# A split that keeps its first half in DRAM, and a close that loads it

## The chip, the cores and the metric

The kernel runs on one core of one Trainium2 chip. The metric is the device time of one launch in microseconds (us), lower is better; runs of one kernel are compared by their median.

## The reference, cut to what matters

The input is four images of 96 channels by 128 x 128 pixels (NCHW, float32). Layer 0 is a group norm followed by a selective-scan block (a 1 x 1 convolution to 192 channels, a depthwise 3 x 3, SiLU, four scans in different directions, a layer norm over channels, a 1 x 1 convolution back), added to the input. Layer 1 is the part that the change touches:

```python
def _relu_split_norm(x, sc1, sc2, res_coef, nc1, nc2):
    x = x - mean(x);  x1 = relu(x);  x2 = x - x1
    ...                                   # masks, pos, neg, avg1, avg2
    x1n = sqrt(pos/total) * _layer_norm(x1 + avg1 * downmask)
    x2n = sqrt(neg/total) * _layer_norm(x2 + avg2 * upmask)
    out = 0.5 * (nc1 * x1n + nc2 * x2n) + res_coef * x
    return (out, sc1 * x1 + x1n, sc2 * x2 + x2n)

xr, x1, x2 = _relu_split_norm(_gn(x), ...)
y1 = _layer_norm(_attn_conv(x1, x2, aw1, aw2, aw3))
y2 = _layer_norm(_conv2d(x2, w_conv2, 1)) * x1
x = x + xr + _conv2d(concat([y1, y2]), w_full, 0) + b_full
```

`_attn_conv` makes keys from `x1`, queries from `x2`, a softmax over them as 3 x 3 convolution weights, and convolves a value map of `x1` with those. The first half `x1` is so needed twice: as the input of the convolutions, and at the end as the factor of `y2`.

## The kernel before

The scans of layer 0 come first. After them the images go one by one through four steps, each a Python generator that emits instructions and yields the cost it estimates for them:

- `norm`: the end of layer 0 for the image. It writes the image's new `x` to DRAM (`xnew`, 96 x 16384) in 16 pieces of 96 x 1024.
- `split` (`split_norm`): loads `xnew` once for the sums, then again in 16 pieces. For each piece and each half, ScalarE makes scale times x plus shift (L1253) and VectorE masks it by the threshold `thr` (L1257). For images 1 to 3 the result stands in a tile `half` of 8 rows x 4 column groups x 33 (32 pixels and one pad of zero, 96 x 1056 floats; two tiles for the first half, one for the second). From it six planes are made on ScalarE and GpSimd (first half) or VectorE (second half) and stored to `x1p` and `x2p`. Only the planes are kept, not the half. For image 0 the two halves themselves are stored, as maps with one pad per row of 129 (`x1d`, `x2d`). There the pixels stand in plain order; the planes of the other images split a row into four groups of 32, and all that follows for them stands in that order (`img.mapped` tells the two apart).
- `attend`: the convolutions and the attention of the image, in strips of 12 rows on TensorE (`products`, L1467 and L1482), with ScalarE copies (L1540, L1928) and VectorE combinations (L1554 to L1562). It stores the `w_conv2` convolution to `c2d` and the attention's output to `od`. Its inputs `ya`, `yc` are loaded two strips ahead (L1903, L1911).
- `close` (`attn_output`): 16 pieces of 96 x 1024. It loads `od` (tile `o`), `c2d` (tile `c2`) and `xnew` (tile `xx`) one piece ahead, makes the first half again from `xx` in tile `x1` (`first_half`: L2273 on ScalarE, L2274 on VectorE), forms (c2 - mean) * x1 in place (L2316), makes the residual `e` (`residual`: L2278 on ScalarE, L2279 and L2280 on VectorE), multiplies both by the 1 x 1 weights (L2324, L2325), adds `e` into `x1` (L2327 or L2329) and stores `x1` to the output (L2331). Every tile of it has two buffers.

`co_run(left, right, pace)` interleaves the emission of `attend` (left) with a chain of lighter work (right): beside `attend` of image b run `norm` and `split` of image b+1 and `close` of image b-1. Beside the last image runs `close` of image 2 with its yields doubled, and then `LastOutput`, which does for image 3 what `close` does in three steps. `before` makes `x1` and `e` of image 3 from `xnew` and stores both (`x1s`, `es`); `beside` loads them with `c2d` and adds the second product into a tile that stays; `after` adds the first product and stores the output.

All loads and stores named here are issued by SyncE (SP), in its program's order, except the stores of `x1d` and `x2d`. After the scans, the order of instructions on each engine is that of a scheduler in the framework, which moves instructions of attention, split and close past each other; within an engine each instruction waits for its place in that order.

Of the kernel before, what the change touches and what calls it, by code (L numbers as in the profile page):

```python
# [9 lines left out]
F32 = mybir.dt.float32  # L10
BF16 = mybir.dt.bfloat16
AF = mybir.ActivationFunctionType
ALU = mybir.AluOpType
# [4 lines left out]
C = 96  # L18
H = W = 128
L = H * W  # L20
# [9 lines left out]
PW = W + 1  # L30
TW = 4
NP = TW + 2
TN = W // TW
PB = TN + 1
PP = PB * TW
# [18 lines left out]
SN = 1024  # L54
NS = L // SN
RS = SN // W
# [15 lines left out]
def kernel(  # L72
# [26 lines left out]
    nc = tc.nc  # L99
# [4 lines left out]
    dram = ctx.enter_context(tc.tile_pool(name="dram", bufs=2, space=DRAM))  # L104
# [983 lines left out]
                    nc.sync.dma_start(xnew[:, bass.ts(old, SN)], near.pop(old)[turned])  # L1088
                yield 1.4

    def split_norm(xnew, x1d, x2d, stats, keep, cnt, ps, side, planes, vector, done):


        with ExitStack() as pools:
            p4 = pools.enter_context(tc.tile_pool(name="n4", bufs=3, side=side))
            ahead = []
# [13 lines left out]
            m = col("m1")  # L1110
# [12 lines left out]
            t = col("t1")  # L1123
# [6 lines left out]
            later = Later()  # L1130
            p1 = ExitStack()
            p2 = p1.enter_context(tc.tile_pool(name="n1", bufs=2, side=side))
            for i in range(NS):
                y = ahead.pop(0)
# [80 lines left out]
            def stored(i, m, h):  # L1215
                if planes:
                    def then(pl):
                        store_planes(nc.sync, m, i * RS, RS, pl)
                        done[m is x2d] = (i + 1) * RS

                    return planes_of(later, p2, h, RS, then, vector=vector(i, m is x2d))
                at = (i * RS + 1) * PW
                return lambda: nc.scalar.dma_start(m[:, at : at + RS * PW], h)

# [1043 lines left out]
        nc.gpsimd.memset(y[C : C + 1], 1.0)  # L2268
        return y[0 : C + 1]

    def first_half(img, xx, x1):
        thr, scale, shift = (img.keep[n] for n in ("thr", "scale", "shift"))
        nc.scalar.activation(x1, xx, AF.Identity, scale=scale[:, 0:1], bias=shift[:, 0:1])  # L2273
        nc.vector.scalar_tensor_tensor(x1, xx, thr, x1, ALU.is_gt, ALU.mult)  # L2274

    def residual(img, xx, e):
        up, low, thr = (img.keep[n] for n in ("up", "low", "thr"))
# [4 lines left out]
    def pixels(v):  # L2282

        return v.rearrange("p (h j t) -> p h t j", j=TW, t=TN)

    def plain(v):
        return v.rearrange("p (h t j) -> p h t j", j=TW, t=TN)

    def attn_output(img, ps, side, share):
        ob = out[img.b].rearrange("c h w -> c (h w)")  # L2290
        with (
            tc.tile_pool(name="f1", bufs=1, side=side) as p1,
            tc.tile_pool(name="f3", bufs=2, side=side) as p3,
        ):
            w1 = own_weights(img, ps, p1)
            s2, w2 = c2_weights(img, ps, p1)
            ones = [with_ones(p1, f"o{i}") for i in range(2)]

            def loads(t):
                o = ones[t % 2]  # L2300
                got = [o]
                nc.sync.dma_start(o[0:C], img.od[:, bass.ts(t, SN)])
                for name, src in (("c2", img.c2d), ("xx", img.xnew)):
                    y = p3.tile([C, SN], F32, name=name)
                    nc.sync.dma_start(y, src[:, bass.ts(t, SN)])
                    got.append(y)
                return got

            ahead = loads(0)
            for t in range(NS):  # L2310
                o, c2, xx = ahead
                if t + 1 < NS:
                    ahead = loads(t + 1)
                x1 = p3.tile([C, SN], F32, name="x1")
                first_half(img, xx, x1)
                nc.vector.scalar_tensor_tensor(  # L2316
                    c2, c2, s2[0:C, 0:1], x1, ALU.subtract, ALU.mult
                )
                e = p3.tile([C, SN], F32, name="e")
                residual(img, xx, e)  # L2320
                for h in range(2):
                    sl = bass.ts(h, CH)
                    pf = part(ps, C, CH)
                    nc.tensor.matmul(pf, lhsT=w1, rhs=o[:, sl], start=True, stop=False)  # L2324
                    nc.tensor.matmul(pf, lhsT=w2, rhs=c2[:, sl], start=False, stop=True)  # L2325
                    if img.mapped:
                        nc.vector.tensor_add(x1[:, sl], pf, e[:, sl])  # L2327
                    else:
                        nc.vector.tensor_add(plain(x1[:, sl]), pixels(pf), pixels(e[:, sl]))  # L2329
                    yield 2.6 * share  # L2330
                nc.sync.dma_start(ob[:, bass.ts(t, SN)], x1)  # L2331

    class LastOutput:

# [3 lines left out]
        def __init__(self, img, ps, side):  # L2338
            self.img, self.ps, self.side = img, ps, side
            self.pools = ExitStack()  # L2340
            self.kept = None
            self.x1d, self.ed = (dram.tile([C, L], F32, name=n, bufs=1) for n in ("x1s", "es"))

        def open(self):
            pool = self.pools.enter_context(tc.tile_pool(name="o3", bufs=1, side=self.side))
# [3 lines left out]
        def before(self):  # L2349

            img = self.img
            self.open()
            with tc.tile_pool(name="f3", bufs=2, side=self.side) as p3:
                def load(t):
                    y = p3.tile([C, SN], F32, name="xx")
                    nc.sync.dma_start(y, img.xnew[:, bass.ts(t, SN)])
                    return y

                ahead = load(0)
                for t in range(NS):  # L2360
                    xx = ahead
                    if t + 1 < NS:
                        ahead = load(t + 1)
                    x1, e = (p3.tile([C, SN], F32, name=n) for n in ("x1", "e"))
                    first_half(img, xx, x1)
                    yield 4.0
                    residual(img, xx, e)
                    yield 5.2
                    for d, y in ((self.x1d, x1), (self.ed, e)):
                        nc.sync.dma_start(d[:, bass.ts(t, SN)], y)  # L2370

        def beside(self):

            img = self.img
            while self.kept is None:
                yield None
            with (
                tc.tile_pool(name="f1", bufs=1, side=self.side) as p1,
                tc.tile_pool(name="f3", bufs=2, side=self.side) as p3,
            ):  # L2380
                s2, w2 = c2_weights(img, self.ps, p1)

                def loads(t):
                    got = []
                    for name, src in (("c2", img.c2d), ("x1", self.x1d), ("e", self.ed)):
                        y = p3.tile([C, SN], F32, name=name)
                        nc.sync.dma_start(y, src[:, bass.ts(t, SN)])
                        got.append(y)
                    return got

                ahead = loads(0)
                for t in range(NS):
                    c2, x1, e = ahead
                    if t + 1 < NS:
                        ahead = loads(t + 1)
                    nc.vector.scalar_tensor_tensor(
                        c2, c2, s2[0:C, 0:1], x1, ALU.subtract, ALU.mult
                    )
                    for h in range(2):
                        sl = bass.ts(h, CH)  # L2400
                        pf = part(self.ps, C, CH)
                        nc.tensor.matmul(pf, lhsT=w2, rhs=c2[:, sl], start=True, stop=True)
                        nc.vector.tensor_add(
                            plain(self.kept[:, t, sl]), pixels(pf), pixels(e[:, sl])
                        )
                        yield 2.2
# [29 lines left out]
    class Image:  # L2436


        def __init__(self, b):
            self.b = b  # L2440
            self.xnew = dram.tile([C, L], F32, name="xnew", bufs=3)
            self.x1p, self.x2p, self.vp = planes[b % 2]
            self.x1d, self.x2d, self.vd = maps if b == 0 else (None, None, None)
            self.stats = istats[b % 2].tile([C, NCH, 6], F32, name="xstats", tag="xstats")
            self.cnt = istats[b % 2].tile([C, 5, NS], F32, name="cnt", tag="cnt")
            self.keep = {}
            self.mapped, self.lifting = False, False
            self.done = [0, 0]
            self.finished = False
            self.last = None  # L2450
            self.maps_made = lambda: None
            self.watd = None if b else dram.tile([C, 3, NP, C], F32, name="watd", bufs=1)
# [13 lines left out]
        def split(self, ps, side, vector=lambda i, second: False):  # L2466
            halves = (self.x1p, self.x2p) if self.b else (self.x1d, self.x2d)
            yield from split_norm(
                self.xnew, *halves, self.stats, self.keep, self.cnt, ps, side, self.b > 0, vector,
                self.done,  # L2470
            )

# [215 lines left out]
```

## Time and profile before

| | |
|---|---|
| median of 3 runs | 6464.88 us (6458.56 to 6468.28) |
| time of the profiled execution | 6470.83 us |
| its span, first to last instruction | 6468.9 us |
| TensorE matmul (PE) busy | 5321.3 us, 82% |
| VectorE (DVE) busy | 4711.2 us, 73% |
| ScalarE (ACT) busy | 3786.8 us, 59% |
| GpSimd (POOL) busy | 3238.6 us, 50% |
| DMA | 1205.18 MB, 186 GB/s |
| mean granted TensorE clock | 0.889 |

Busy time is the sum of the times of an engine's instructions; the idle time of an engine is put down to the instruction or transfer that ended it. "DMA share" is the mean busy share of the 16 DMA engines in a stretch, and GB/s is what they moved in it. The granted clock is a share of the full one. A share over the whole span is a mean over stages of very different kind, so the stages are read one by one.

### The profile page before, as it was taken

Reading aid. Unit: us, or ns where it says so; the run is one execution under the profiler, and the core shown is the slowest. Engines: PE = TensorE matmul, PEld = TensorE weight load, DVE = VectorE, ACT = ScalarE, POOL = GpSimd, SP = SyncE. Lnnn points to the kernel's source line nnn. Section 1 sums busy time; section 2 is a strip of 40 time slices with the busy share of each in tenths; the row PEclk is TensorE's granted clock in tenths of the full one; section 3 lists DMA queues with packets and bytes.
Section 4 is the critical chain, followed back from the end, with each engine's and each line's share of the span. In section 5 each row is a group of like instructions: output and inputs, shape, how many; then the busy total and the mean of one; then the engine's idle time right before and its main releaser. Section 6 shows DMA issues by size and latency. Waiting matters only on the chain. (4 is left out here: it accounts for less than half of the span.)

```text
span 6468.9 us, 76257 instructions
## 1 busy us (share of the span) xinstructions
PE 5321.3 (82%) x23264; PEld 2301.3 (36%) x23264; DVE 4711.2 (73%) x7132; ACT 3786.8 (59%) x4770; POOL 3238.6 (50%) x2472
## 2 busy tenths in 40 slices
PE   6889988987888753989988588877888877989888
PEld 2333323322222111444433234345333445345553
DVE  4247778988989668988934785468874587888757
ACT  1247767776787676777632565466533665545642
POOL 1226757978889544979821344346213266022310
PEclk9999989998998665999999799888988988999989
DMA  6767777775675766675666776665766655966668
GB/s 154 176 157 193 191 202 196 218 213 163 199 198 163 214 173 215 197 217 174 199 182 185 187 220 161 164 157 155 213 195 164 178 145 155 243 174 181 191 170 219
DMA packets 891433, 1205.18 MB, mean 186 GB/s; under 512 B 228533, under 2 KB 743483, under 8 KB 878545
## 3 DMA queue, kind: packets, MB, share of 16 engines
q1 hardware_dynamic: 860496, 1145.35, 65.2%
q0 software_dynamic: 16208, 38.41, 2.2%
q10 hardware_dynamic: 14320, 16.54, 0.9%
q8 instruction: 187, 3.06, 0.2%
q14 instruction: 222, 1.81, 0.1%
HBM read 777.82 MB, written 345.62 MB: 174 GB/s over the span
## 5 line engine op out<-in xcount | busy, mean ns | idle before, releaser
L629 PE MATMUL bank<-y,wp 128*128 128x512 f32 (+3 forms) x3584 | 1320.2, 626 | 84.5 <-DMA y<-y 40.9
L862 POOL TENSOR_TENSOR y<-y,dl 128x1024 f32<-128x1024 f32 x384 | 1062.5, 2767 | 273.1 <-DVE dl L854 247.9
L829 POOL TENSOR_TENSOR dl<-dl,u 128x1024 f32<-128x1024 f32 x384 | 1015.8, 2645 | 247.1 <-ACT dA L805 129.5
L850 DVE TENSOR_TENSOR_SCAN dA<-dA,pBC 128x512 f32<-128x512 f32 x768 | 981.6, 1278 | 30.7
L1467 PE MATMUL two<-ya,wd 128*64 128x192 f32 (+3 forms) x2376 | 590.6, 422 | 201.7 <-ACT odd L1540 77.1
L629 PEld LDWEIGHTS bank<-y,wp 128*128 128x128 f32 (+3 forms) x3584 | 459.3, 169 | 755.8 <-issue 658.0
L854 DVE TENSOR_TENSOR dl<-dA,pBC 128x512 f32<-128x512 f32 x768 | 528.4, 688 | 260.0 <-PE pBC L743 187.1
L2159 PE MATMUL bank<-y,wn 128*64 128x384 f32 (+5 forms) x2408 | 665.2, 501 | 52.7 <-DMA y<-x1d 28.3
L743 PE MATMUL pBC<-xr,wbc 60*128 60x512 bf16 (+1 forms) x1536 | 458.5, 405 | 301.3 <-DVE dA L850 230.9
L1928 ACT COPY yb<-ya 64x768 f32<-64x768 f32 (+1 forms) x660 | 537.5, 814 | 202.6 <-PE two L1467 128.7
L672 ACT ACTIVATE dl<-pd,dtb 128x512 f32<-128x512 f32 x768 | 486.3, 684 | 183.2 <-PE pd L743 166.8
L1467 PE MATMUL two<-yb,wd 128*64 128x192 f32 (+3 forms) x2376 | 566.4, 407 | 4.0 <-ACT yb L1928 4.0
L833 DVE TENSOR_TENSOR pBC<-dl,pBC 128x512 f32<-128x512 f32 x768 | 527.5, 687 | 8.1 <-POOL dl L829 7.1
L2159 PEld LDWEIGHTS bank<-y,wn 128*64 128x64 f32 (+3 forms) x2408 | 306.9, 167 | 340.2 <-issue 150.9
L805 ACT ACTIVATE dA<-dl,negA 128x1024 f32<-128x1024 f32 x384 | 420.3, 1142 | 2.3
L1467 PEld LDWEIGHTS two<-ya,wd 128*64 128x64 f32 (+1 forms) x2376 | 266.9, 169 | 399.5 <-ACT odd L1540 87.8
L672 ACT ACT_TABLE_LOAD x248 | 318.2, 1283 | 94.9 <-PE pd L743 81.6
L743 PEld LDWEIGHTS <-wbc 60*128 60x128 bf16 (+1 forms) x1536 | 102.9, 96 | 749.3 <-issue 736.1
L1467 PEld LDWEIGHTS two<-yb,wd 128*64 128x64 f32 (+1 forms) x2376 | 295.1, 170 | 153.6 <-issue 41.5
L1012 PE MATMUL bank<-y,outws 96*96 96x512 f32 x512 | 313.6, 752 | 11.4 <-DVE r L1025 8.7
L1467 PE MATMUL two<-ya,wa 128*96 128x384 f32 (+1 forms) x528 | 229.9, 519 | 72.1 <-DMA ya<-vp 27.4
L1540 ACT COPY odd<-two 128x384 f32<-128x384 f32 (+5 forms) x176 | 116.0, 659 | 286.7 <-PE two L1482 177.2
(316 smaller groups left out, 9210.2 us busy)
## 6 DMA issues: line engine op xcount, KB each, us to landing
u<-zb SPq DMA_DIRECT2D x192, 1024.0 KB
yms<-y SPq DMA_DIRECT2D x96, 512.0 KB
y<-yms SPq DMA_DIRECT2D x64, 768.0 KB
xn<-xnew SPq DMA_DIRECT2D x128, 384.0 KB
ya<-vp SPq DMA_DIRECT2D x120, 336.0 KB
y<-y SPq DMA_DIRECT2D x128, 258.2 KB
zb<-z SPq DMA_DIRECT2D x64, 512.0 KB
ya<-x1p SPq DMA_DIRECT2D x90, 336.0 KB
```

Of the source, the lines that this page charges most:

```text
L629: nc.tensor.matmul(blocks(pz[p:e]), lhsT=ws[k][:, d, c : c + e - p], rhs=window(ys[k], at, d, n), start=(i == 0), stop=(i == len(terms) - 1),)
L672: nc.scalar.activation(dst, src, AF.Softplus, bias=bias)
L743: nc.tensor.matmul(p, lhsT=w[rows], rhs=xr[rows, at : at + CH], start=True, stop=True)
L805: nc.scalar.activation(live[m]["dA"], live[m]["dl"], AF.Exp, scale=negA[:, g % 3, k : k + 1])
L829: nc.gpsimd.tensor_mul(t, t, u_view(n))
L833: nc.vector.tensor_mul(p, live[n]["dl"][:, bass.ts(half, CH)], p)
L850: nc.vector.tensor_tensor_scan(h, h, p, init, ALU.mult, ALU.add)
L854: nc.vector.tensor_mul(live[n]["dl"][:, sl], live[n]["dA"][:, sl], live[n]["C", half])
L862: nc.gpsimd.tensor_add(v, v, t.rearrange("p (a b) -> p a b", b=W))
L1467: nc.tensor.matmul(of(to[p:e], r), lhsT=w[:, i, c : c + e - p], rhs=tiles(t[k][PAIR[i]][:, SLOT[i]], o, r), start=(k == 0), stop=False,)
L1928: nc.scalar.copy(yb[k][64 * h - 64 : 64 * h, :, :n], ya[k][0:64, :, h * TN : h * TN + n])
L2159: nc.tensor.matmul(pc[p:e, :n].rearrange("p (h w) -> p h w", w=W), lhsT=w[:, c : c + e - p], rhs=v[:, :, 0:W], start=(i == 0), stop=(i == ...
```

## The change

`split` of images 1 to 3 stores the tile `half` of the first half, pads and all, to a new DRAM tensor `x1h` (one DMA of 96 x 1056 floats a piece), just ahead of the instructions that make its planes. `close` no longer calls `first_half`, which is gone: it loads the piece of the first half from `x1h`, or for image 0 from the map `x1d` that is stored already (96 x 1032 floats), as a fourth load one piece ahead, and reads it through a view that leaves the pads out. The sum goes to a tile `to` of its own. `LastOutput.before` makes and stores `e` alone, without the yield of 4.0 that stood behind `first_half`; `beside` loads the first half from `x1h` in place of `x1s`.

```diff
@@ split_norm
-                    return planes_of(later, p2, h, RS, then, vector=vector(i, m is x2d))
+                    made = planes_of(later, p2, h, RS, then, vector=vector(i, m is x2d))
+
+                    def kept_too():
+                        nc.sync.dma_start(x1h[:, bass.ts(i, RS * PP)], h)
+                        made()
+
+                    return made if m is x2d else kept_too
@@
-    def first_half(img, xx, x1):
-        thr, scale, shift = (img.keep[n] for n in ("thr", "scale", "shift"))
-        nc.scalar.activation(x1, xx, AF.Identity, scale=scale[:, 0:1], bias=shift[:, 0:1])
-        nc.vector.scalar_tensor_tensor(x1, xx, thr, x1, ALU.is_gt, ALU.mult)
+    def first_rows(img, pool, t):
+        if img.mapped:
+            y = pool.tile([C, RS * PP], F32, name="x1")[:, : RS * PW]
+            nc.sync.dma_start(y, img.x1d[:, (t * RS + 1) * PW : (t * RS + RS + 1) * PW])
+            return y.rearrange("p (h w) -> p h w", w=PW)[:, :, 1:PW]
+        y = pool.tile([C, RS * PP], F32, name="x1")
+        nc.sync.dma_start(y, img.x1h[:, bass.ts(t, RS * PP)])
+        return y.rearrange("p (h b) -> p h b", b=PB)[:, :, 0:TN]
+
+    def less_mean(c2, s2, x1):
+        v = c2.rearrange("p (h b) -> p h b", b=x1.shape[2])
+        nc.vector.scalar_tensor_tensor(v, v, s2[0:C, 0:1], x1, ALU.subtract, ALU.mult)
@@ attn_output
-                return got
+                return got + [first_rows(img, p3, t)]
...
-                o, c2, xx = ahead
+                o, c2, xx, x1 = ahead
...
-                x1 = p3.tile([C, SN], F32, name="x1")
-                first_half(img, xx, x1)
-                nc.vector.scalar_tensor_tensor(
-                    c2, c2, s2[0:C, 0:1], x1, ALU.subtract, ALU.mult
-                )
+                less_mean(c2, s2, x1)
+                to = p3.tile([C, SN], F32, name="to")
...
-                        nc.vector.tensor_add(x1[:, sl], pf, e[:, sl])
+                        nc.vector.tensor_add(to[:, sl], pf, e[:, sl])
...
-                nc.sync.dma_start(ob[:, bass.ts(t, SN)], x1)
+                nc.sync.dma_start(ob[:, bass.ts(t, SN)], to)
@@ LastOutput.before
-                    x1, e = (p3.tile([C, SN], F32, name=n) for n in ("x1", "e"))
-                    first_half(img, xx, x1)
-                    yield 4.0
+                    e = p3.tile([C, SN], F32, name="e")
                     residual(img, xx, e)
                     yield 5.2
-                    for d, y in ((self.x1d, x1), (self.ed, e)):
-                        nc.sync.dma_start(d[:, bass.ts(t, SN)], y)
+                    nc.sync.dma_start(self.ed[:, bass.ts(t, SN)], e)
@@ LastOutput.beside
-                    for name, src in (("c2", img.c2d), ("x1", self.x1d), ("e", self.ed)):
+                    for name, src in (("c2", img.c2d), ("e", self.ed)):
...
-                    return got
+                    return got + [first_rows(img, p3, t)]
@@ Image.__init__
+            self.x1h = dram.tile([C, H * PP], F32, name="x1h", bufs=3) if b else None
```

More of the change, by code (lines that the diff above doesn't have):

```diff
@@ L1089, in ssm_output, with split_norm @@
                 yield 1.4
-    def split_norm(xnew, x1d, x2d, stats, keep, cnt, ps, side, planes, vector, done):
+    def split_norm(xnew, x1d, x2d, x1h, stats, keep, cnt, ps, side, planes, vector, done):
         with ExitStack() as pools:
@@ L2326, in attn_output @@
                     if img.mapped:
-                        nc.vector.tensor_add(x1[:, sl], pf, e[:, sl])
+                        nc.vector.tensor_add(to[:, sl], pf, e[:, sl])
                     else:
-                        nc.vector.tensor_add(plain(x1[:, sl]), pixels(pf), pixels(e[:, sl]))
+                        nc.vector.tensor_add(plain(to[:, sl]), pixels(pf), pixels(e[:, sl]))
                     yield 2.6 * share
-                nc.sync.dma_start(ob[:, bass.ts(t, SN)], x1)
+                nc.sync.dma_start(ob[:, bass.ts(t, SN)], to)
     class LastOutput:
@@ L2341, in __init__ @@
             self.kept = None
-            self.x1d, self.ed = (dram.tile([C, L], F32, name=n, bufs=1) for n in ("x1s", "es"))
+            self.ed = dram.tile([C, L], F32, name="es", bufs=1)
         def open(self):
@@ L2388, in loads @@
                         got.append(y)
-                    return got
+                    return got + [first_rows(img, p3, t)]
                 ahead = loads(0)
                 for t in range(NS):
-                    c2, x1, e = ahead
+                    c2, e, x1 = ahead
                     if t + 1 < NS:
                         ahead = loads(t + 1)
-                    nc.vector.scalar_tensor_tensor(
-                        c2, c2, s2[0:C, 0:1], x1, ALU.subtract, ALU.mult
-                    )
+                    less_mean(c2, s2, x1)
                     for h in range(2):
@@ L2468, in split @@
             yield from split_norm(
-                self.xnew, *halves, self.stats, self.keep, self.cnt, ps, side, self.b > 0, vector,
+                self.xnew, *halves, self.x1h, self.stats, self.keep, self.cnt, ps, side,
+                self.b > 0, vector,
                 self.done,
```

## The prediction

> **What bounds the kernel now.** The page's first part gives every engine room, so the whole span tells nothing here; I looked for the lines of the change by tile (`xx`, `e`, `half`, `x1s`) and cut the span into the stages in which they run.
>
> ```profile
> PE 5321.3 (82%) x23264; PEld 2301.3 (36%) x23264; DVE 4711.2 (73%) x7132; ACT 3786.8 (59%) x4770; POOL 3238.6 (50%) x2472
> ...
> L2274 DVE SCALAR_TENSOR_TENSOR x<-xx,kept,x 96x1024 f32<-96x1024 f32 x64 | 83.7, 1307 | 51.2 <-ACT x L2273 32.3 <-DMA od<-own 12.8 <-DMA o<-od 2.9
> L2273 ACT ACTIVATE x<-xx,kept 96x1024 f32<-96x1024 f32 x64 | 79.3, 1240 | 34.2 <-DMA xx<-xnew 21.3 <-DMA out<-x 12.1 <-DMA o<-od 0.5
> ```
>
> The two removed rows are 83.7 us of VectorE and 79.3 us of ScalarE. Next, the busy time by stage. The columns after the stretch are its length, then busy us and count of PE, weight loads, DVE, ACT and POOL, the granted clock, the DMA share and GB/s:
>
> ```profile
> 3650.00:3700.00 50.00, 19.55 (x65) 9.05 (x65) 37.97 (x64) 23.13 (x31) 22.66 (x31) 0.66 0.78 205
> 4680.00:4811.00 131.00, 102.39 (x286) 37.62 (x286) 111.93 (x126) 50.72 (x50) 12.73 (x13) 0.84 0.69 195
> 5150.00:5500.00 350.00, 270.80 (x1863) 173.54 (x1859) 286.53 (x571) 210.14 (x297) 212.99 (x312) 0.84 0.58 152
> 5515.00:5705.00 190.00, 168.13 (x554) 70.24 (x552) 172.18 (x217) 101.67 (x117) 0.12 (x1) 0.96 0.88 236
> 5705.00:5970.00 265.00, 240.57 (x1344) 128.54 (x1344) 215.18 (x313) 121.21 (x149) 76.33 (x98) 0.95 0.66 172
> 5970.00:6160.00 190.00, 165.33 (x1236) 104.57 (x1228) 151.44 (x237) 117.17 (x144) 62.69 (x87) 0.96 0.68 190
> 6160.00:6235.00 75.00, 66.96 (x527) 44.81 (x528) 38.17 (x88) 39.17 (x57) 25.69 (x52) 0.94 0.62 152
> ```
>
> The rows from 4680, 5515 and 5705 are the closes of images 0, 1 and 2, 5970 is `before` of image 3, 3650 and 5150 hold splits. In the first two closes VectorE is the busiest engine (85% and 91%), and in the second the DMA engines follow at 0.88. Inside that close, by tens of microseconds (same columns):
>
> ```profile
> 5535.00:5545.00 10.00, 9.05 (x28) 3.65 (x27) 9.05 (x11) 6.14 (x8) 0.00 (x0) 1.00 1.05 272
> 5545.00:5555.00 10.00, 8.16 (x30) 2.96 (x29) 9.86 (x12) 7.64 (x10) 0.00 (x0) 1.00 1.04 283
> 5555.00:5565.00 10.00, 9.05 (x32) 3.95 (x33) 8.97 (x12) 6.02 (x7) 0.00 (x0) 1.00 1.02 293
> 5565.00:5575.00 10.00, 9.03 (x30) 3.58 (x28) 9.30 (x14) 4.89 (x6) 0.00 (x0) 1.00 1.03 275
> ```
>
> A share of 1.02 to 1.05 at 272 to 293 GB/s: 281 GB/s is what the DMA engines carry there when they have no gap. Last, the waits of TensorE:
>
> ```profile
> PE two L1467 <- DMA ya<-vp: 27.4, 2, 27.2
> ```
>
> That one wait, at 3652 to 3680, is for the value planes of image 0, and the first split runs beside it.
>
> **The change, part by part.** Counts come from the instruction order of the changed program: VectorE and ScalarE have 64 instructions less each, SP has 80 DMAs more (48 stores of `x1h`, 48 more loads, 16 stores of `x1s` less), the rest is the same but stands in another order from the first split on. One transfer of 96 x 1056 floats is 0.4055 MB, 1.44 us at 281 GB/s.
>
> Close of image 0 (131 us). Before, seven of its pieces share 4680 to 4743 (63 us) with 54 attention matmul instructions, four run alone (7.5 us each, 4743 to 4773), and five share 38 us with 24 more. After, the scheduler puts 54 attention instructions among the first five pieces and leaves eleven alone; the other 24 come behind the close. Their price is 0.46 us (36.5 us of L1467 and L1482 in this window over 79 instructions), 11 us. The five mixed pieces: 63 us, less two pieces at 7.5 us, less a little of five times 1.3 us: 47 us. A piece alone needs on VectorE 3 x 1.3 + 2 x 0.68 = 5.2 us, with the idle 1.0 us of before 6.2; on the DMA engines five transfers in place of four, 1.97 MB, 7.0 us at 281 GB/s; 7.9 us at 250. The loads of a piece now all stand on SP behind the store of the piece two before it, so I take 7.1: 47 + 11 x 7.1 + 11 = 136 us, **+5** (6.2: -5; 7.9: +14). The instruction that goes (20.5 us of L2274 in this stage) is on the path, but the fourth load takes its place.
>
> Close of image 1 (190 us). Off VectorE go 15 x 1.27 = 19 us. The DMA engines were busy 0.88 x 190 = 167 us and get 16 x 1.44 = 23 us more: 190 us without one gap. The nearest long row is 0.94 (5515 to 5625); at 0.95 the stage takes 200 us, **+9** rounded down for stores that may slip behind it. The other end: if the loads find room, two thirds of VectorE's 19 us come back, since TensorE is busy 168 of 190 us and also waits for ScalarE: -12. The upper end is +14, at a share of 0.93. What waits then is L2316 for its load, at the head of VectorE's queue, with attention's L1554 to L1562 behind it, and TensorE behind those for its PSUM tiles.
>
> [...]
>
> Close of image 2 (265 us) and `before` (190 us). VectorE loses 22.0 and 22.1 us (17 and 16 instructions of L2274, 1292 and 1384 ns), ScalarE some 20 each. DMA at 0.66 has room for 23 us; in `before` it loses 16 stores. TensorE is busy 91% and 87%, so at most 24 and 25 us are there; a quarter of VectorE's relief reaches it: **-5** (0 to -15). In `before` the light work shrinks from 9.2 to 5.2 units a piece, so it ends earlier, and some 64 of 147 units of attention run as in the row from 6160 (89% busy against 87%): 2 us, and half as much again for ScalarE and VectorE each: **-4** (0 to -14). The removed stall (L2274 for ScalarE, 32.3 us) stays: L2279 now waits for L2278, which waits for the same load.
>
> First split, beside image 0's value planes. VectorE's new order has three more L1257 (0.74 us) and the rest of one plane set (2.6 us, 3666.8 to 3669.5) ahead of the last value plane, and `x1h` stores stand before its store on SP. The wait of 27.2 us grows by up to 5; the work done early is missing later, where VectorE is 88% busy: **+4** (0 to +8).
>
> The 48 stores cost 69 us of DMA time in splits at 0.58 to 0.78. On SP each waits for L1257, as the next load of `xn` does anyway; behind it stand `ya` loads that are two strips ahead. I take **+4** for contention (0 to +12; a gain is excluded, since nothing is removed there). The pads cost VectorE nothing: L1257 already works on rows of 32 with a step of 33, at 736 ns for 512. `beside` swaps one load for one 3% larger.
>
> Sum: 5 + 9 - 5 - 4 + 4 + 4 = +13 us on the profiled execution's 6470.83 (span 6468.9 and 1.9 around it): 6484. That execution was 6 us above the median, so the same step from 6464.88 gives **6478 us**.
>
> **The rivals.** *VectorE's time comes back* (34%). DMA carries the fourth load, as the 293 GB/s row suggests: close 1 gives -12, close 0 -5, the last two -10 and -8, the splits +8: -27 us, 6438. It decides from a piece of close 0 under 6.6 us (47 + 6.6 x 11 + 11 = 131). For it: VectorE hardly idles in close 1. Against it: the DMA rows above 1.0.
>
> *The parts cancel* (24%). Close 1 at 0, the splits at +4 in all: 13 - 9 - 4 = 0, 6465.
>
> *SP as the bound* (8%, within the slower side). If a third of the 48 stores hold SP for 3.8 us (72.3 us in 19 waits of its `xn` loads for L1257) and half of that reaches TensorE through `ya`: 30 us more, 6508.
>
> That the instructions do not go away is excluded by the order.
>
> **How the numbers follow.** My forecast with its worse variant has 42%: slower by over 0.2%, which is 13 us and about what a measurement of this kernel can tell from no change. The range reaches from the fast rival, 6 us beyond, to the SP case: 6432 to 6508; the likeliest case alone spans 6470 to 6500.
>
> **What would show it.** Right: close 0 with bare pieces of 7 us or more, DMA share near 1.0 through close 1 and VectorE waiting at L2316's successor for the `x1h` load, VectorE some 84 us less busy, the wait for `ya<-vp` above 27 us. Wrong: bare pieces of 6.2 us, close 1 shorter than 185 us at over 290 GB/s, or TensorE waiting for `ya` beside the splits.

## The result, and the profile after

The changed kernel is slower: 6542.50 us median of four runs (6537.61 to 6552.06) against 6461.72 us of four runs of the kernel before beside it (6450.66 to 6468.28), a ratio of 1.0126 with a 95% interval of 1.0108 to 1.0143, or +81 us. The forecast had the sign and missed the size: 6478, with an upper end of 6508. The profiled execution took 6543.28 us, its span 6541.5 us.

The first part of the page of the changed kernel:

```profile
PE 5362.6 (82%) x23264; PEld 2307.5 (35%) x23264; DVE 4638.7 (71%) x7068; ACT 3714.6 (57%) x4706; POOL 3230.4 (49%) x2472
```

VectorE and ScalarE lost 72.5 and 72.2 us of work, of the 84 and 79 that went with their two instructions, and the kernel lost 81 us of time. TensorE is 41 us *more* busy with the same 23264 instructions. So something keeps TensorE waiting and slows it. The busy time by stage of the changed kernel (columns as in the prediction: length, PE, weight loads, DVE, ACT, POOL, granted clock, DMA share, GB/s). The rows are split 1, split 2, close 0, split 3, close 1 and close 2:

```profile
3600.00:3907.00 307.00, 219.57 (x935) 108.08 (x931) 262.11 (x434) 179.39 (x244) 144.61 (x178) 0.84 0.76 209
4340.00:4642.00 302.00, 239.33 (x1408) 139.07 (x1407) 246.15 (x451) 184.57 (x254) 170.31 (x244) 0.85 0.67 185
4711.00:4841.00 130.00, 94.49 (x236) 32.56 (x235) 89.69 (x100) 25.70 (x26) 0.25 (x2) 0.82 0.84 230
5192.00:5508.00 316.00, 235.89 (x1650) 150.74 (x1646) 253.28 (x445) 178.92 (x252) 190.93 (x269) 0.87 0.59 164
...
5556.00:5778.00 222.00, 188.12 (x568) 76.72 (x568) 159.36 (x208) 85.49 (x102) 0.23 (x2) 0.89 0.86 231
5790.00:6039.00 249.00, 229.03 (x1342) 123.33 (x1341) 182.71 (x268) 100.92 (x130) 68.56 (x96) 0.97 0.75 195
```

The same stages of the kernel before, from a second profile of it that was taken among the experiments (label e12_before_again; splits 1, 2, 3 and close 1):

```profile
3587.00:3880.00 293.00, 204.90 (x887) 101.08 (x883) 260.81 (x431) 176.77 (x240) 133.42 (x173) 0.84 0.73 197
4301.00:4584.00 283.00, 223.35 (x1388) 133.67 (x1387) 246.69 (x440) 180.04 (x248) 175.88 (x246) 0.87 0.64 172
5145.00:5440.00 295.00, 234.69 (x1640) 152.23 (x1635) 244.77 (x445) 178.09 (x248) 191.94 (x269) 0.86 0.59 155
5486.00:5683.00 197.00, 173.99 (x571) 72.80 (x570) 178.59 (x225) 104.38 (x120) 0.23 (x2) 0.96 0.84 228
```

The three splits are longer by 14, 19 and 21 us in these rows, close 1 by 25. Read the row of close 1: VectorE has 19 us less to do and the DMA share (0.86) is hardly above before's (0.84), so neither is the bound. The granted clock of TensorE fell from 0.96 to 0.89. Busy time times clock is 174.0 x 0.96 = 167 before and 188.1 x 0.89 = 167 after: by these products the work is the same, and an estimate from them puts 14 us of the stage on the lower clock and the other 11 on gaps. What VectorE and TensorE wait for in close 1 of the changed kernel (5556 to 5772 us; us in total, times, longest):

```profile
DVE e L2295 <- ACT e L2294: 28.5, 7, 9.1
DVE to L2342 <- PE bank L2338: 26.4, 16, 5.9
...
PE bank L2338 <- DVE c L2290: 19.6, 7, 4.6
```

The same waits in the kernel before (5513 to 5711 us; there VectorE waits at L2274 for ScalarE's first instruction of a piece):

```profile
DVE x L2329 <- PE bank L2325: 12.0, 9, 2.8
...
DVE x L2274 <- ACT x L2273: 1.0, 1, 1.0
...
PE bank L2325 <- DVE c L2316: 3.7, 2, 2.9
```

In the changed kernel three engines wait for each other: VectorE for ScalarE's `e`, which stands behind attention's copies; TensorE for VectorE's `c`; VectorE for the products. For the load of `x1h`, which the forecast named, VectorE waits 4.7 us in the whole run. The wait ahead of attention's first products, 27.2 us before, is now

```profile
PE two L1473 <- DMA wa<-watd: 22.0, 1, 22.0
```

so the first split does not delay it. A second wait for value planes, of 4.2 us, comes 27 us later.

### The profile page after: what moved, and what is told of

It reads as the page before. It is cut to its first block, busy times and chain, and to the rows that moved or that the text cites. A ratio compares the mean times of both kernels' runs of the same rounds, so it can differ in the third digit from the quotient of the medians.

```text
span 6541.5 us, 76155 instructions
## 1 busy us (share of the span) xinstructions
PE 5362.6 (82%) x23264; PEld 2307.5 (35%) x23264; DVE 4638.7 (71%) x7068; ACT 3714.6 (57%) x4706; POOL 3230.4 (49%) x2472
```

## The experiments

All ratios are against runs of the kernel before that were taken beside them. That kernel's median was 6442 to 6462 us over those chips, and the part up to split 1, which no edit touches, took 3585 to 3609 us in the profiles, so stages tell more than totals. In the table a split goes from the start of an image's first masking instruction (L1257 in the kernel before) to that of its last, a close from its first product with `od` to its last with `c2`, and the last stage from the end of close 2 to attention's 7920th product of 8712 (`before` of image 3 lies in it); all read from the trace, in us. "Old order" is explained at the second pair.

| kernel | splits 1, 2, 3 | close 1 | close 2 | to 7920th | ratio (95%) |
|---|---|---|---|---|---|
| before | 294, 283, 295 | 197 | 242 | 210 | |
| before, again (e12) | 293, 283, 295 | 197 | 242 | 207 | 0.9998 (0.9983 to 1.0012) |
| changed | 306, 302, 316 | 222 | 249 | 205 | 1.0126 (1.0108 to 1.0143) |
| e1 stores alone | 306, 297, 316 | 200 | 242 | 211 | 1.0099 (1.0084 to 1.0114) |
| e2 small stores | 300, 300, 316 | 194 | 242 | 211 | 1.0065 (1.0048 to 1.0082) |
| e5 stores, old order | 312, 313, 300 | 199 | 241 | 208 | 1.0092 (1.0068 to 1.0117) |
| e6 their order, no store | 310, 300, 315 | 200 | 240 | 210 | 1.0077 (1.0057 to 1.0098) |
| e13 small stores, old order | 310, 310, 302 | 199 | 241 | 204 | 1.0099 (1.0084 to 1.0115) |
| e9 stores by ScalarE, old order | 303, 287, 293 | 199 | 242 | 210 | 1.0030 (1.0019 to 1.0041) |
| e3 loads alone | 294, 284, 297 | 217 | 247 | 202 | 1.0045 (1.0026 to 1.0064) |
| e4 one load more | 295, 282, 291 | 229 | 251 | 217 | 1.0109 (1.0092 to 1.0126) |
| e7 the same, old order | 295, 283, 297 | 203 | 242 | 210 | 1.0014 (1.0000 to 1.0028) |
| e8 change, old order | 312, 313, 301 | 195 | 230 | 195 | 1.0053 (1.0034 to 1.0071) |
| e10 e8, stores by ScalarE | 306, 287, 292 | 195 | 228 | 193 | 0.9987 (0.9975 to 0.9999) |
| e11 change, stores by ScalarE | 301, 290, 300 | 220 | 245 | 206 | 1.0070 (1.0057 to 1.0083) |
| e14 images 2 and 3, as e10 | 294, 286, 292 | 199 | 231 | 192 | 0.9977 (0.9967 to 0.9988) |
| e15 the same, planner's order | 299, 293, 299 | 199 | 245 | 188 | 1.0006 (0.9992 to 1.0019) |

The repeated profile of before agrees with the first within 2 us in every split and in closes 1 and 2. Close 0 (129.7 and 133.2 us) and the last column (210 and 207) differ by 3 us or more:

> The kernel before itself, as one of the runs, for its stages on the chip that the experiments ran on and for how far two profiles of one program differ. Every theory: the time of before within 10 us, the splits at 294, 282 and 294 us and close 1 at 197 us, each within 4 us.

### The stores alone, full and small

```diff
+                        nc.sync.dma_start(x1h[:, bass.ts(i, RS * PP)], h)                # e1
+                        nc.sync.dma_start(x1h[:, bass.ds(i * RS * PP, 8)], h[:, 0:8])    # e2
                         made()
```

> The kernel before with the 48 stores of x1h in split and nothing else: the closes make the first half again, nobody reads x1h. In the changed kernel the shift against before grows by 12 us over split 1, by about 20 us over split 2 and by about 33 us over split 3 on TensorE's attention instructions, and by 26 us in close 1; close 0 gives nothing.
> Theory S (the stores and the order they bring carry most of the loss): the three splits lengthen as in the changed kernel, close 1 stays within 5 us of the 190 us of before; time +40 to +50 us, 6502 to 6512.
> Rival C (the closes carry it, and the growth in the splits comes from work that the changed closes push around): the splits lose under 10 us in all, time +0 to +12 us.
> The forecast's own terms (first split +4, stores +4): +8 us, 6470.

> As the stores alone, but each of the 48 stores takes 8 of the 1056 floats of a partition (48 x 3 KB in place of 48 x 0.4055 MB), so the DMA instructions and what they wait for on SP stay and 19.3 MB go. The planned order is near that of the full stores but not the same (114 of 16953 rows of TensorE's order differ).
> If the bytes cost (48 x 1.44 us of all DMA engines): the time goes back to within 8 us of before, 6458 to 6473.
> If the place of the stores on SP and the order cost: within 10 us of the kernel with the full stores, some 6495 to 6515.

The 48 stores with nothing else cost 61 us (6502.43 against 6441.57), 47 us of it in the three splits; the closes stay as they were. The small stores cost 42 us and 45 us in the splits, though they move 1/132 of the bytes. So the bytes are at most a part, and the small stores' time lies between the two that were expected. But both had a new order of instructions on every engine from split 1 on, so what costs could still be a store or the order that came with it.

### The stores and the order, one without the other

From the end of the scans on, the order on each engine is the planner's. To hold a kernel to another's order, each instruction is tied behind the one that stood ahead of it on its engine in that other program (an edge that orders issue and waits for nothing):

```diff
+    as_listed(listed, ORDER)   # per engine, for each pair (last, at) of the listed order:
+    #   tc.add_manual_dep(t[at], t[last].name, DependencyInfo(NoSync, DATA), ...)
```

Instructions that the other program lacks are left to the planner. Held to the order of before, the kernel with the stores has before's order row by row on TensorE, VectorE, ScalarE and GpSimd, and 48 new places on SP.

> The kernel before with the 48 full stores of x1h, and with the order of instructions on every engine held to that of before (from the end of the scans on, each instruction is tied behind the one that stood ahead of it on its engine in before's planned program). Only the 48 stores are new, at 48 places of SP's order; the planned orders of TensorE, VectorE, ScalarE and GpSimd are those of before, row by row. With the planner's own new order the same stores cost 61 us (6502 against 6442).
> Theory O (the planner's new order costs, not the stores): time within 12 us of before, the splits 1, 2 and 3 within 4 us each of 294, 282 and 294 us.
> Theory B (the stores themselves cost, by their bytes or by what waits behind them on SP): +40 us or more, splits 2 and 3 at 300 and 316 us.

> The other half of the pair: the kernel before without any store, held to the order that the planner made for the kernel with the 48 stores. On TensorE, VectorE, ScalarE and GpSimd it is that kernel's order row by row, SP's is that less the stores.
> Theory O: it loses what the kernel with the stores lost, +40 to +61 us, with splits 2 and 3 at about 300 and 316 us.
> Theory B: within 12 us of before.

Theory O falls for the stores: in the old order they cost 60 us as well (splits 312, 313, 300). And the planner's order costs 51 us with no store in it. The two do not add: with the stores the new order loses 47 us in the splits, without them 54. In the planner's order, with the stores, VectorE does not wait for `x1h<-half` at all; that order avoids the stores' waits and pays as much for it. Which of its waits make up the price was not taken apart. The waits that it avoids are in the trace of the stores in the old order (line numbers are those of that kernel, L1445 is the masking instruction, L2099 a load of attention). First VectorE's wait over the whole run, then its part in split 1 and in split 2:

```profile
DVE half L1445 <- DMA x1h<-half: 45.4, 8, 11.2
...
DVE half L1445 <- DMA x1h<-half: 18.9, 4, 10.8
...
DVE half L1445 <- DMA x1h<-half: 26.2, 3, 11.2
```

In split 3 it is 0.2 us. The splits lose 18, 31 and 6 us, so the loss is where this wait is. SP's own longest wait in split 2:

```profile
SPq L2099 <- PE two L1670: 52.2, 9, 14.3
```

VectorE may not write a tile `half` again before its store has read it, and the store stands on SP behind loads that wait for attention. SP also waits at the stores themselves (38.5 us for the masking in this run, by split 19.5, 2.0 and 17.1), but the losses do not follow that. In that kernel a store is issued 17, 21 and 15 us (mean of splits 1, 2, 3; up to 51) after its tile is written, and in the changed kernel 23, 24 and 27 us. A piece of split 2 takes 18 us and there are two tiles. A third tile was not tried. While L1445 waits, attention's instructions wait behind it on VectorE: in split 1 TensorE waits 19.0 us for VectorE's `own`, against 1.8 before. The small stores in the old order separate this hold from the bytes:

> The kernel before with the 48 small stores (8 of 1056 floats of a partition) issued by SP, held to before's order: the same instructions in the same places as the full stores from SP in that order (+60 us; splits 312, 313, 300 us), up to a few places in SP's order, with 19.3 MB less to move.
> Theory W (the tile is held until the store has had its turn on SP): it loses nearly as much, +35 to +60 us, and VectorE's L1257 waits for x1h<-half as it did.
> Theory B (bytes): within 12 us of before.

They cost the same (splits 310, 310, 302), and the wait is there as with the full ones:

```profile
DVE half L1445 <- DMA x1h<-half: 40.9, 6, 10.2
```

### The stores from another engine

```diff
-                        nc.sync.dma_start(x1h[:, bass.ts(i, RS * PP)], h)
+                        nc.scalar.dma_start(x1h[:, bass.ts(i, RS * PP)], h)
```

> The kernel before with the 48 stores, held to before's order, but the stores are issued by ScalarE in place of SP; in ScalarE's order most stand right ahead of ScalarE's own first read of the same tile. From SP the same stores in the same order cost 60 us, and VectorE waited 26 us in split 2 for x1h<-half before it could write the tile again.
> Theory W (the two tiles are held too long, because the store stands on SP behind waits for attention): the wait of L1257 for x1h<-half goes, splits at 294, 282 and 294 us within 6 us each, time within 15 us of before.
> Theory B (the bytes: 19.5 MB more in stages at a DMA share of 0.6): the splits stay at 312, 313 and 300 us, +40 us or more.

ScalarE reads the same tile for the planes anyway, and most stores come right ahead of that read; they are issued 1.0 to 1.7 us after the tile is written. VectorE has no wait for `x1h` any more, and the loss in the splits falls from 54 to 13 us with the same bytes and the same order of everything else. Of these 13, split 1 has 9. There TensorE's two waits for `ya<-vp` take 37.1 us against 27.4 before, the second of them 9.7 against 0.2; just ahead of that load SP waits 7.3 us at loads of weights for stores of `x1h` to land. Why those loads wait for the stores is not shown. In total the kernel is 1.0030 of before, 23 us against 6447.21, 8 us more than the 15 that theory W allowed.

Issued by ScalarE, the stores cost the splits 42 us less, and VectorE's wait of 45.4 us went; to start a store takes SP 0.4 us in the median of the 48 in the changed kernel, 33 us for all of them. What counted here was where the store stands: on SP behind loads that wait for attention (52.2 us in split 2), on ScalarE mostly right ahead of its read of the tile.

### The closes

```diff
# e3: the changed kernel without the stores; what it loads in place of x1h is xnew
-        nc.sync.dma_start(y, img.x1h[:, bass.ts(t, RS * PP)])
+        nc.sync.dma_start(y, img.xnew[:, bass.ds(min(t * SN, L - RS * PP), RS * PP)])
# e4, e7: the kernel before, in loads(t) of attn_output
+                y = p3.tile([C, RS * PP], F32, name="more")
+                nc.sync.dma_start(y, img.xnew[:, bass.ds(min(t * SN, L - RS * PP), RS * PP)])
```

> The changed kernel without its 48 stores: the closes of images 1 to 3 load 96 x 1056 floats of xnew where the changed kernel loads x1h (so this kernel leaves the first half of images 1 to 3 out of the last product), image 0 loads x1d as in the changed kernel. Up to close 0 the order is that of before, instruction by instruction.
> Theory S+L (two separate losses): nothing lost up to close 0; close 0 within 8 us of 131; close 1 at 205 to 218 us as in the changed kernel (216); close 2 and before about +5 to +15: time +20 to +40 us, 6482 to 6502.
> Rival C (closes carry all of it): +60 us or more.
> The forecast's terms without its stores and first split: +5 us, 6467, with the DMA share of close 1 at 0.95 and VectorE waiting for the x1 load.

> The kernel before, whose closes make the first half again as they did, with one more load of 96 x 1056 floats a piece (out of xnew, into a tile that nobody reads): the transfer of the changed kernel without its other edits. It tells whether close 1 is long for its bytes.
> DMA theory (the forecast's reason for close 1: 0.88 of 190 us and 23 us of transfers more): close 1 at 200 us or more, with a DMA share of 0.93 or more, close 0 +5 or more: time +15 to +35 us.
> Rival Q (the loss of close 1 is in the queue order: the instruction L2294 on ScalarE stands behind attention's copies and VectorE's first two instructions of a piece wait for it): close 1 within 6 us of 190 us, the DMA share between 0.95 and 1.0; time within 10 us of before.

> The kernel before with one load of 96 x 1056 floats more in each piece of the closes, held to before's order; only the 48 loads are new in SP's order. With the planner's own order it cost 67 us (6509 against 6442) and close 1 took 229 us in place of 197 (first product to last).
> Theory O: close 1 within 8 us of 197, the time within 15 us of before.
> DMA theory (the forecast's: 23 us of transfers more than close 1 has room for): close 1 at 205 us or more, at a DMA share of 0.93 or more; +10 to +30 us in all.

> The changed kernel (with the yield of 4.0 in LastOutput.before kept, so that its steps come in the same sequence) held to the order of before on every engine: what the change removed is out, its 48 stores and 64 loads stand where the planner puts them on SP, everything else is row by row as in before.
> Theory O: the loss goes, 80 us less than the changed kernel and within 20 us of before; if VectorE's 84 us and ScalarE's 79 us are worth anything on the path, below before: close 1 at 190 us or less, total -10 to -30 us.
> Theory B and DMA theory: +40 us or more of the 81 us stay, with close 1 at 210 us or more.

The loads alone cost 29 us, close 1 at 217; with the stores' 61 that makes 90 against 81. One load more, with the recomputation kept, cost 67 us, more than either expectation had, and made close 1 longer still (229), which looked like the DMA theory and against rival Q. But its DMA share was no higher than before (0.83 against 0.84), and its wait is the same one under the old name (window of close 1, then VectorE's wait in it):

```profile
5492.00:5722.00 230.00, 190.01 (x588) 77.02 (x580) 180.51 (x228) 105.24 (x120) 0.23 (x2) 0.91 0.83 222
```

```profile
DVE x L2274 <- ACT x L2273: 28.8, 6, 8.8
```

The same program in the old order settles it: 203 us for close 1, 11 us over before in all, of which close 0 has 5 to 8 (138 us). And the whole change in the old order has a close 1 of 195 and a close 2 of 230 us (the two stages' windows):

```profile
5574.00:5769.00 195.00, 173.77 (x571) 72.88 (x570) 159.97 (x209) 87.84 (x104) 0.24 (x2) 0.96 0.96 262
5782.00:6012.00 230.00, 215.84 (x1256) 116.55 (x1255) 175.65 (x257) 99.05 (x125) 69.61 (x94) 0.97 0.80 212
```

With every transfer of the change, the DMA engines hold 0.96 and 262 GB/s for 195 us, and the stage is 2 us shorter than before. So all 25 us of the changed kernel's close 1 lie in the order. In total the change in the old order is still 36 us over before, more than theory O allowed: the splits lose 54 us as with the stores alone, and close 2 and the stretch behind it gain 12 and 15. Where in the order close 1 loses can be counted on TensorE in part. A piece has four products with `od`, which wait for no arithmetic, and then four with `c2`, which wait for VectorE; attention's products between them can cover that wait. In the old order 14 of 15 pieces have 10 or more between them; in the planner's order for the change 5 of 15, and three have none; with one load more 8 of 15. The count is no measure of the loss, since the stage is longer at 8 than at 5 (229 against 222 us), and no run changes it alone. In the old order the same instructions of the changed kernel (here with the stores by ScalarE, close 1) wait

```profile
DVE to L2522 <- PE bank L2518: 27.9, 14, 4.3
DVE e L2475 <- ACT e L2474: 4.5, 2, 2.6
...
PE bank L2518 <- DVE c L2470: 1.7, 1, 1.7
```

28.5 us of VectorE for ScalarE have become 4.5, and 19.6 of TensorE for VectorE 1.7. Why the planner leaves the old order when a load is added is not shown by any run.

### The parts put together

> The changed kernel held to before's order, with the stores issued by ScalarE. Held to that order with the stores on SP it lost 54 us in the three splits and gained 12 us in close 2 and some 15 us from there to the end of before.
> Theory W: the splits are back within 6 us each, the gains of the closes stay: -10 to -25 us against before.
> Theory B: no better than with the stores on SP, +36 us.

> The changed kernel with one edit: the store of x1h is issued by ScalarE in place of SP; the order is the planner's own. It tells whether the mended store is enough without the old order.
> If the planner's new order in the splits came from the stores on SP: the splits lose under 15 us in all, close 1 stays at 215 to 225 us: +25 to +40 us against before.
> If any store makes the planner leave the old order: +60 us or more, as in the changed kernel (+81).

The change in the old order with the stores by ScalarE is 7 us faster than before (6440.33 against 6447.21; the interval just excludes 1), less than the 10 to 25 expected, with split 1 at 306. The mended store without the old order still loses 45 us: close 1 at 220. That is more than the +25 to +40 expected for it; the splits lose 19 us, where under 15 were expected. Split 1 gives back nothing for its store, since close 1 hardly gains, so the last version has it for images 2 and 3 alone:

```diff
+                return got + ([first_rows(img, p3, t)] if img.b > 1 else [None])
...
+                if x1 is None:      # images 0 and 1: first_half as before, into `to`
```

> The change for images 2 and 3 alone, held to before's order, stores issued by ScalarE: images 0 and 1 make the first half again. From the stages of the runs before: split 1 loses its 13 us and close 0 its 4 us, close 1's 2 us go, split 2 keeps +5, close 2 and before of image 3 keep -14 and -14: 6425 against 6447, -0.25% to -0.4%.
> Rival: split 1's loss moves elsewhere (the stores of image 1 cost what the freed VectorE gives back only later): no better than the whole change in that order, -7 us.

> The same edit (images 2 and 3 alone, stores issued by ScalarE) with the order left to the planner, which is what a plain edit of the source would give.
> Theory O (each edit buys a new order, and the old one was a good one): slower than the same program in the old order by 15 us or more, 6440 to 6475.
> Rival: the planner's order was bad only where the fourth load stands in close 1 and the stores on SP; without both it is within 8 us of the version in the old order.

In the old order it has the lowest ratio of the study (its interval overlaps that of e10): 6448.08 against 6462.05 us, 14 us (0.12% to 0.33%), somewhat under the 22 expected: close 2 and the stretch behind it gave 11 and 15 to 18 us, split 2 took 3, and attention behind the 7920th product took 6 back. With the planner's order the same edit is no different from before (6465.09), 17 us slower than in the old order.

## Why the prediction was right or wrong

**The stores, +4 (0 to +12).** This is the step that failed most: 52 us in the three splits. The working was "On SP each waits for L1257, as the next load of `xn` does anyway", which asks what the store waits for and what stands behind it. It did not ask who waits for the store, and it put the new order of the instructions, which it names, at nothing. The tile has two buffers, the store ends its use, and SP reached it 23 to 27 us late. In the old order VectorE waits 45 us for that; in the changed kernel it does not wait for the store, and the loss comes by the order, which costs 51 us without any store. With the stores on ScalarE the change in the planner's order loses 19 us in the splits in place of 52. That nothing but a loss was possible was right. The bytes, by which the term was sized, cost nothing that a run shows: in the old order 1/132 of them cost as much (splits 310, 310, 302 against 312, 313, 300). The third rival, SP as the bound, had the right engine but the wrong direction for the changed kernel, where SP waits 11 us at the stores: SP held the stores.

**Close 1, +9 (-12 to +14).** Measured +25. The reason was wrong: not the DMA engines, which carried the same transfers in less time in the old order (262 GB/s over 195 us against 231 over 222). The step that failed is the assumption that the order of the close stays as good when its parts change. The program's order was to be had before the run, and the count of products between the two groups there would have been a warning.

The other end of the forecast's range, -12, was for loads that find room. In the old order they found it: -2, at a share of 0.96 and 262 GB/s. So the stage did not grow at this share, but VectorE's freed time was not worth 12. What kept it at 2 is not shown: TensorE is busy 174 of 195 us, and ScalarE's waits for loads in the stage grew from 13 to 33 us.

**First split beside image 0's value planes, +4.** Measured 0: attention's first product starts 73.5 us after the first masking instruction before (73.3 in the second profile), 73.3 us after the change. The wait shrank to 22.0 and did not grow. A growth of such waits did show where ScalarE issued the stores in the old order, by 10 us.

**Close 0, +5.** About right in size. From its first product to its last it measured 128.1 us, against 129.7 and 133.2 in the two profiles of before; but the forecast also counted the 24 attention instructions that come behind it. Up to attention's 3385th product, the last that stood in the close before, it is 139.6 against 130.5 and 135.4: +4 to +9. The eleven bare pieces took 7.8 us each (forecast 7.1), the five mixed ones 43 us (47). That the DMA engines set the price of a bare piece is not shown: there VectorE waits 20.0 us for ScalarE's `e` and for no load.

**Close 2, -5, and `before`, -4.** Measured +6 and, to the 7920th product, -5. The changed kernel's close 2 holds 925 matmuls of attention where before's holds 865, so the two stages are better taken together: from attention's 6070th product to its 7920th it is 461 us against 455 and 451 before, and 427 (e8) and 422 (e10) in the old order. There close 2 and the stretch behind it are -12 to -14 and -15 to -17, near the fast end of the one range (-15) and past that of the other (-14): the relief of VectorE and ScalarE is worth more than I allowed, and the planner's order took it back.

So the forecast's direction was right by terms that were mostly not, which is luck in the main: the sum had +13, of which the two that decided (52 and 25 of the 81 us) were sized for transfers, and what cost were places in queues. Of the first rival's gain 7 to 14 us were there too, with the stores on ScalarE and in an order that the change did not get.

## What to carry to other kernels

Where a DMA is added that reads a tile, ask when its queue will reach it and who must wait to write that tile again, before asking for its bytes; issue it from an engine that reads the tile at that moment anyway (here 54 us lost in the splits became 13). Where a scheduler sets the order, an edit buys a new order for everything around it, and that can cost more than the edit (here 67 us with one load more, and 11 for the same load in the old order); hold the old order and run the edit in it before blaming the hardware. When a stage grows while its busiest engine has less to do (close 1: 25 us longer with 19 us less on VectorE), look at the independent work between a producer and the instruction that waits for it.

## What was not expected of the hardware

The granted clock of TensorE was low beside its gaps. In close 1 it stands at 0.50 in seven stretches of the changed kernel, 48 us in all, and in four of the kernel before, 17 us in all; each begins inside a gap of TensorE or within 1 us behind one. The clock was 0.89 against 0.96 in the mean, to which the estimate above gives 14 of the 25 us. In the kernel before the four gaps are 2.9 to 3.6 us long; in the changed kernel four of them are 3.4 to 4.6 us, two are 3.0 and one is 1.9 us, going by the ends of matmuls that the profile models. After that last one, for example:

```profile
5616.00:5622.00 6.00, 5.98 (x8) 2.38 (x9) 5.05 (x7) 0.72 (x1) 0.00 (x0) 0.50 0.77 182
```

How the clock depends on the length of a gap is not shown by any run. The DMA engines held 262 GB/s for 195 us at a share of 0.96, while the same stage in another order, with the same transfers, moved 231 over 222 us.
